# A hand-written order for the second layer, the last norms of the first layer beside it, and first transposes across row tiles

## The chip, the core and the metric

The kernel runs on one core of a Trainium2 chip. The metric is device time in microseconds (us) of one execution, and the median of several runs is quoted. Engines are named as in the profile: PE is the matrix engine (PEld its weight loads), DVE the vector engine, ACT the scalar (activation) engine, POOL the general engine, SP the engine that only issues transfers here. [...]

## What is computed

Two graph layers over N = 2708 nodes with 256 features in float32. The reference, cut to what matters:

```python
# layer 0: two steps (n = 0, 1), Xf = Xa = X at first
A  = top_p_attention(Xa, W1, W2, W3)      # row softmax, cut to the largest 90%, N x N
Xf = R @ Xf                               # R = (adj + I), rows scaled to sum 1: the "walk"
Xa = A @ Xa                               # the attention
Z  = Z + Xf @ U1[n].T + Xa @ U2[n].T
h  = X + Z;  layer0 = layernorm(h) * ln_g + ln_b
x  = layernorm(x + layer0)
# layer 1: graph attention with 4 heads of 64 features
Wh = einsum('nd,hdo->nho', x, W)          # values
e  = leaky_relu(s_i[:, None] + s_j[None]) # from Wh and a
P  = softmax over j of e where adj[i, j] != 0 (diagonal always)
x  = layernorm(x + einsum('ijh,jho->iho', P, Wh))
```

## The kernel before

**Row tiles.** The 2708 rows are cut into NT = 22 tiles: 16 of 128 rows and 6 of 110. Inside an attention row they are taken in six `groups` (four of 4 tiles with 128 rows, then 4 and 2 tiles with 110 rows).

**Layer 0** (`fast_layer0`, its main part from L1073) is written in an order fixed by hand: inside `tc.manual_schedule` the instructions of PE, ACT, DVE and POOL keep the order of the program. `step(s, ...)` runs over the 22 row tiles of step s. For each one `weigh` (L202) multiplies the attention row tile `e` with the values: for every group it transposes the group's blocks of `e` (L212, on PE), copies them from PSUM to SBUF (L218, on ACT, tile `eT`), and multiplies (L227, tile `att`). The transposes of group n+1 are issued ahead of the matmuls of group n, so that the copy has time; at the start of each row tile, though, groups 0 and 1 are transposed one after the other and the first matmul follows at once. After each group `slot` is called. A slot advances the searches under way (`search`: scores, threshold, candidates, the kept part of `e`, which ends with the DVE instruction of L805), may begin the search of the tile three further on, advances the small chains in `doing`, and pays out `spend` matmuls of the walk (L863). In step 0 spend is 0; in step 1 it is 6 or 7 for each slot. Between the steps thirteen slots of 7 walk matmuls start the searches of step 1.

**The end of a row in layer 0** is `finish` (L931): four sums on POOL into a tile `hh`, then two layernorms (bn_stats and bn_aggr on DVE, L948 and L949; epsilon and power on POOL, L952 and L953; scaling on DVE, L955), with gain, bias and residual on POOL between them (L961 to L963). Then `sources` transposes the row (L141), multiplies it with the weights of layer 1 (L147) and makes the factors `sb`, `tj`, `s_src` and the values `v`, which go to DRAM. Each `yield` in these generators hands over to the next slot.

**The verdict** (L1090 to L1134) is a chain of some 20 small DVE instructions on [128, 22] tiles that tests whether the fast search was exact. It ends in one PE matmul (L1131) and a flag `bad`, read at the very end.

**Layer 1** (`layer1`, L1145) has no order by hand; a planner places its instructions. The 22 target tiles are taken in three spans g (8, 8 and 6 tiles, 1024, 1024 and 660 columns). For each span it runs over all 22 source tiles j. One j is: load a block of the adjacency (L1170), ACT Sign and Square (L1171, L1176) to make a 0/1 mask, for a j inside the span two POOL operations on the diagonal block (L1174, L1175), four DVE instructions, one for each head, that give the weights `pt` (L1233), and on PE eight matmuls with 64 columns for the values (L1241) and eight with 32 columns for the denominators (L1248). `pt` has two buffers for each head. At the end of a span the sums go to SBUF (`val`, `den`), and `settle` (L1179) is called while the next span is at its third j: for all 8 (6) tiles of the span in one go, transposes (L1186, L1187), reciprocal (L1189) and product with it (L1193) on DVE, the residual on POOL (L1198), and `layernorm` (L124 to L132).

Of the kernel before, what the change touches and what calls it, by code (L numbers as in the profile page):

```python
# [8 lines left out]
F32 = mybir.dt.float32  # L9
BF16 = mybir.dt.bfloat16  # L10
I32 = mybir.dt.int32
AF = mybir.ActivationFunctionType
# [32 lines left out]
def kernel(  # L45
# [69 lines left out]
    bad = const.tile([1, 1], I32, name="bad")  # L115

# [19 lines left out]
    def sources(t, pool, ps):  # L136

        m = rows[t]
        tp = ps.tile([P, 4, P], F32, name="tr")
# [5 lines left out]
        wp = ps.tile([P, 4, P], F32, name="tr").rearrange("p a b -> p (a b)")  # L145
# [14 lines left out]
        nc.sync.dma_start(vd[t][:m], vt[:m])  # L160

# [40 lines left out]
    def weigh(acc, e, m, value, pool, ps, copies, between=None):  # L202

        def turned(n):
            grp = groups[n]
            tr = ps.tile([P, 4, P], F32, name="tr")  # L210
            for q, t in enumerate(grp):
                nc.tensor.transpose(  # L212
                    tr[: rows[t], q, :m], e[:m, off[t] : off[t + 1]], ident[:m, :m]
                )
            eT = pool.tile([P, 4, P], F32, name="eT")
            copy = copies[n % len(copies)]
            k = rows[grp[0]]
            copy(eT[:k, : len(grp), :m], tr[:k, : len(grp), :m])  # L218
            return eT

        ahead = turned(0)
        for n, grp in enumerate(groups):
            eT = ahead
            if n + 1 < len(groups):
                ahead = turned(n + 1)
            for q, t in enumerate(grp):
                nc.tensor.matmul(  # L227
                    acc, eT[: rows[t], q, :m], value(t),
                    start=(t == 0), stop=(t == NT - 1),
                )  # L230
            if between:
                between(n)


    def general_layer0():
        with ExitStack() as l0:
# [6 lines left out]
            g_sb = w0.tile([P, D], F32, name="g_sb")  # L243
            b_sb = w0.tile([P, D], F32, name="b_sb")
# [8 lines left out]
            nc.scalar.dma_start(g_sb, ln_g.partition_broadcast(P))  # L253
            nc.scalar.dma_start(b_sb, ln_b.partition_broadcast(P))
# [153 lines left out]
            def attend(t, e, rden, cur, dst):  # L408

                m = rows[t]  # L410
                ac = ps_ac.tile([P, CHUNK], F32, name="ac")
                weigh(ac[:m, :D], e, m, lambda j: cur[: rows[j], j, 0:D],
                      tpp, ps_tr, [nc.scalar.copy])
                nc.scalar.activation(dst, ac[:m, :D], AF.Copy, scale=rden[:m])
# [74 lines left out]
            for t in range(NT):  # L489
                for _ in sources(t, rowp, ps_tr):  # L490
                    pass


    def fast_layer0(ep, adjp):
# [24 lines left out]
        g_sb = w0.tile([P, D], F32, name="g_sb")  # L519
        b_sb = w0.tile([P, D], F32, name="b_sb")  # L520
# [13 lines left out]
        nc.scalar.dma_start(g_sb, ln_g.partition_broadcast(P))  # L534
        nc.scalar.dma_start(b_sb, ln_b.partition_broadcast(P))
        def constant(name, value, width=1):
            c = w0.tile([P, width], F32, name=name)
            nc.gpsimd.memset(c, value)
            return c
# [5 lines left out]
        ones = constant("ones", 1.0)  # L545
        place = w0.tile([P, 8], F32, name="place")
        for k in range(8):
# [5 lines left out]
                constant(f"fact{s}{k}", v, NT)  # L553
# [5 lines left out]
        wants = w0.tile([P, NT, SEGS], F32, name="wants")  # L559
        haves = w0.tile([P, NT, SEGS], F32, name="haves")  # L560
# [263 lines left out]
        def walks():  # L824
# [16 lines left out]
            for n, (s, t, j0, j1) in enumerate(queue):  # L841
# [7 lines left out]
                if j0 == 0:  # L849
                    ac = ps_wk.tile([P, CHUNK], F32, name="walk")  # L850
                    ca = finp.tile([P, D], F32, name="ca", bufs=4)
# [79 lines left out]
        def finish(t, ac, ca, cb):  # L931
# [9 lines left out]
            hh = heldp.tile([P, D], F32, name="hh", bufs=4)[:m]  # L941
            nc.gpsimd.tensor_add(hh, ca[:m], cb[:m])
            nc.gpsimd.tensor_add(hh, hh, held.pop(t)[:m])
            nc.gpsimd.tensor_add(hh, hh, xw)
            yield
            for last in range(2):
                st, mv = small.tile([P, 6], F32, name="ln_st")[:m], small.tile([P, 2], F32, name="ln_mv")[:m]
                nc.vector.bn_stats(st, hh)  # L948
                nc.vector.bn_aggr(mv, st)  # L949
                yield  # L950
                ve, rs = new("ln_ve", m), new("ln_rs", m)
                nc.gpsimd.tensor_scalar(ve, mv[:, 1:2], LN_EPS, None, op0=ALU.add)  # L952
                nc.gpsimd.tensor_tensor(rs, ve, minus_half[:m], op=ALU.pow)  # L953
                yield
                nc.vector.tensor_scalar(  # L955
                    xt if last else hh, hh, mv[:, 0:1], rs, op0=ALU.subtract, op1=ALU.mult
                )
                yield
                yield
                if not last:  # L960
                    nc.gpsimd.tensor_mul(hh, hh, g_sb[:m])  # L961
                    nc.gpsimd.tensor_add(hh, hh, b_sb[:m])
                    nc.gpsimd.tensor_add(hh, hh, ca[:m])  # L963
                    yield
                    yield
            yield from sources(t, rowp, ps_tr)


        engines = {nc.tensor.engine, nc.scalar.engine, nc.vector.engine, nc.gpsimd.engine}
# [25 lines left out]
        def step(s, cur, spend):  # L995
            for t in range(NT):
                m = rows[t]
                e, rden = ready.pop(t)
# [7 lines left out]
                def between(n):  # L1006
                    last = n == len(groups) - 1
                    if last:
# [9 lines left out]
                    slot(spend[n], (s, t + 3) if last else None)  # L1018

                weigh(ac[:m, :D], e, m, lambda j: cur[: rows[j], j, 0:D],  # L1020
                      tpp, ps_tr, [nc.scalar.copy], between)
# [44 lines left out]
        with tc.manual_schedule(engines=engines):  # L1066
# [10 lines left out]
            for t in range(3):  # L1077
                for n in range(6):
                    slot(SPEND_BETWEEN, None if n else (1, t))
                    if t == 2:  # L1080
                        break
# [4 lines left out]

        good = small.tile([P, 2, NT], F32, name="good")
        for s, r in enumerate(sorted_):  # L1090
            z, nxt, most, above, left = facts[s]
            ok, more = good[:, s, :], small.tile([P, NT], F32, name="more")
            nc.vector.tensor_tensor(ok, most, nxt, op=ALU.is_le)
            nc.vector.scalar_tensor_tensor(
                ok, nxt, 0.0, ok, op0=ALU.is_gt, op1=ALU.mult
            )
            if s:
                nc.vector.tensor_tensor(wants, wants, haves, op=ALU.min)
                nc.vector.tensor_reduce(more, wants, axis=AX.X, op=ALU.max)
                nc.vector.scalar_tensor_tensor(  # L1100
                    ok, more, 8.0, ok, op0=ALU.is_le, op1=ALU.mult
                )

                nc.vector.tensor_tensor(more, most, nxt, op=ALU.is_equal)
                nc.vector.tensor_add(above, above, left)
                nc.vector.tensor_scalar(above, above, float(r), None, op0=ALU.is_lt)
                nc.vector.tensor_mul(more, more, above)
                nc.vector.scalar_tensor_tensor(
                    ok, more, 0.0, ok, op0=ALU.is_equal, op1=ALU.mult
                )  # L1110

                nc.vector.scalar_tensor_tensor(
                    ok, left, float(r), ok, op0=ALU.is_lt, op1=ALU.mult
                )
            else:
                nc.vector.tensor_add(more, above, left)
                nc.vector.scalar_tensor_tensor(
                    ok, more, float(r), ok, op0=ALU.is_equal, op1=ALU.mult
                )
            nc.vector.scalar_tensor_tensor(  # L1120
                ok, z, Z_LOW, ok, op0=ALU.is_gt, op1=ALU.mult
            )
            nc.vector.scalar_tensor_tensor(
                ok, z, Z_HIGH, ok, op0=ALU.is_lt, op1=ALU.mult
            )
        total = small.tile([P, 1], F32, name="total")
        nc.vector.tensor_reduce(
            total, good.rearrange("p s t -> p (s t)"), axis=AX.X, op=ALU.add
        )
        pt = ps_wk.tile([P, CHUNK], F32, name="walk")  # L1130
        nc.tensor.matmul(pt[0:1, 0:1], total, ones, start=True, stop=True)  # L1131
        nc.vector.tensor_scalar(
            bad, pt[0:1, 0:1], -1.0, float(2 * NT * P), op0=ALU.mult, op1=ALU.add
        )  # L1134
        l0.close()
        return ahead
# [7 lines left out]
    def layer1(ep, adjp, r):  # L1144
# [9 lines left out]
        first = list(range(GT, NT - 2)) + list(range(GT)) + [NT - 2, NT - 1]  # L1154
# [24 lines left out]
        def settle(g, val, den):  # L1179

            for t in spans[g]:
                m = rows[t]
                cols = slice(off[t] - off[spans[g][0]], off[t + 1] - off[spans[g][0]])
                u = ps_u.tile([P, H, P], F32, name="aux")
                for q in range(2):
                    nc.tensor.transpose(u[:m, q, :], val[:, q, cols], ident)  # L1186
                nc.tensor.transpose(u[:m, 2, :], den[:, cols], ident)  # L1187
# [132 lines left out]
```

## Time and profile before

| | |
|---|---|
| device time, median of 3 runs | 1656.84 us (1656.59 to 1657.43) |
| span of the profiled execution | 1655.3 us |
| busy: PE / DVE / ACT / POOL | 1577.3 / 1229.6 / 742.3 / 430.1 us |
| mean granted PE clock | 0.987 |
| layer 0, step 0: first to last L227 | 78.9 to 468.0 us |
| layer 0, step 1: first to last L227 | 531.4 to about 1253 us |
| first matmul of layer 1 (L1241) | 1274.29 us |
| last matmul of layer 1's sums ends | about 1630.5 us |
| last DVE instruction (L132) | 1645.10 us |

The span counts from the first instruction to the last. "Busy" counts the time in which at least one instruction of the engine was under way. In the PE rows of the time line a float32 matmul shows as two records, so "x16" is eight matmuls. A row of a time line gives the start in us, the length, the engine, the line of the kernel, the operation, output and inputs, and the number of instructions merged into it; "[idle before <-releaser]" is how long the engine had stood idle and whose end let it go on.

### The profile page before, as it was taken

Reading aid. Unit: us, or ns where it says so; the run is one execution under the profiler, and the core shown is the slowest. Engines: PE = TensorE matmul, PEld = TensorE weight load, DVE = VectorE, ACT = ScalarE, POOL = GpSimd, SP = SyncE. Lnnn points to the kernel's source line nnn. Section 1 sums busy time; section 2 is a strip of 40 time slices with the busy share of each in tenths; the row PEclk is TensorE's granted clock in tenths of the full one; section 3 lists DMA queues with packets and bytes.
Section 4 is the critical chain, followed back from the end, with each engine's and each line's share of the span. In section 5 each row is a group of like instructions: output and inputs, shape, how many; then the busy total and the mean of one; then the engine's idle time right before and its main releaser. Section 6 shows DMA issues by size and latency. Waiting matters only on the chain. (4 is left out here: it accounts for less than half of the span.)

```text
span 1655.3 us, 23835 instructions
## 1 busy us (share of the span) xinstructions
PE 1577.3 (95%) x8029; PEld 1035.8 (63%) x8029; DVE 1229.6 (74%) x3682; ACT 742.3 (45%) x1263; POOL 430.1 (26%) x908
## 2 busy tenths in 40 slices
PE   7999999999999999999999999999997999999894
PEld 3476667666677887787778877887773222222332
DVE  3676667666508877876888888987873999899795
ACT  3433444343335555455455655556524344243231
POOL 2200000000022223222225554455433030420313
PEclk9999999999999999999999999999997999999997
DMA  7200000000024333233333433433354333432231
GB/s 196 69 9 15 9 9 11 9 9 8 12 68 121 90 90 98 80 83 78 80 90 97 111 106 99 111 100 91 90 132 143 109 92 97 123 88 80 79 84 32
DMA packets 172493, 128.26 MB, mean 77 GB/s; under 512 B 44342, under 2 KB 161804, under 8 KB 172362
## 3 DMA queue, kind: packets, MB, share of 16 engines
q1 hardware_dynamic: 166442, 115.87, 26.0%
q0 software_dynamic: 3648, 9.26, 1.8%
q10 hardware_dynamic: 2272, 1.52, 0.3%
q8 instruction: 65, 1.06, 0.3%
q14 instruction: 66, 0.54, 0.1%
HBM read 111.78 MB, written 13.46 MB: 76 GB/s over the span
## 5 line engine op out<-in xcount | busy, mean ns | idle before, releaser
L218 ACT COPY eT<-tr 128x512 f32<-128x512 f32 (+5 forms) x264 | 137.7, 539 | 252.0 <-PE tr L212 251.5
L227 PE MATMUL att<-xm,eT 128*128 128x256 f32 (+3 forms) x968 | 229.3, 381 | 17.4 <-ACT eT L218 17.4
L656 ACT ACTIVATE junk<-e,minus,rth 128x2708 bf16<-128x2708 f32 (+1 forms) x88 | 232.8, 2646 | 14.6 <-POOL rth L688 13.7
L227 PE MATMUL att<-ba,eT 128*128 128x256 f32 (+3 forms) x968 | 232.9, 381 | 5.1 <-ACT eT L218 4.9
L1241 PE MATMUL acc<-pt,v 128*64 128x512 f32 (+3 forms) x1056 | 229.3, 555 | 5.7 <-DVE pt L1233 4.5
L863 PE MATMUL walk<-xe,blk 128*128 128x257 f32 (+3 forms) x968 | 223.8, 382 | 1.9 <-DVE xf L877 1.8
L863 PE MATMUL walk<-xm,blk 128*128 128x256 f32 (+3 forms) x968 | 221.8, 380 | 0.0
L1233 DVE SCALAR_TENSOR_TENSOR pt<-e,tj,blk 128x1024 f32<-128x1024 f32 (+3 forms) x176 | 186.5, 1117 | 29.3 <-PE acc L1248 12.5
L863 PEld LDWEIGHTS walk<-xe,blk 128*128 128x128 f32 (+3 forms) x968 | 177.3, 185 | 46.7 <-issue 13.7
L227 PEld LDWEIGHTS att<-xm,eT 128*128 128x128 f32 (+3 forms) x968 | 171.2, 186 | 44.7 <-ACT eT L218 22.2
L863 PEld LDWEIGHTS walk<-xm,blk 128*128 128x128 f32 (+3 forms) x968 | 177.8, 186 | 32.9 <-issue 4.9
L227 PEld LDWEIGHTS att<-ba,eT 128*128 128x128 f32 (+3 forms) x968 | 171.0, 186 | 32.6 <-ACT eT L218 10.2
L635 ACT ACTIVATE e<-lg 128x1024 f32<-128x1024 f32 (+1 forms) x132 | 121.0, 921 | 131.6 <-PE lg L631 131.3
L736 DVE MAX8 cand<-e 128x8 f32<-128x170 f32 (+1 forms) x352 | 89.7, 323 | 114.4 <-ACT e L635 114.3
L1241 PEld LDWEIGHTS acc<-pt,v 128*64 128x64 f32 (+1 forms) x1056 | 72.8, 138 | 158.3 <-issue 112.0
L212 PEld LDWEIGHTS tr<-ident,e 128*128 128x128 f32 (+3 forms) x968 | 113.6, 139 | 45.5 <-PE lg L631 14.5
L212 PE MATMUL tr<-ident,e 128*128 128x128 f32 (+3 forms) x968 | 139.4, 270 | 0.9 <-DVE e L805 0.5
L1171 ACT ACTIVATE blk<-blk 128x1024 f32<-128x1024 f32 (+3 forms) x66 | 63.1, 956 | 165.9 <-DMA blk<-in_adjT_dram 159.5
L1248 PE MATMUL acc<-pt,sb 128*32 128x512 f32 (+3 forms) x1056 | 123.6, 548 | 0.0
L1233 DVE SCALAR_TENSOR_TENSOR pt<-r,tj,blk 128x1024 f32<-128x1024 f32 (+1 forms) x88 | 110.6, 1314 | 8.2 <-issue 5.5
L736 DVE MAX8 cand<-scr 128x8 f32<-128x97 f32 (+1 forms) x616 | 101.7, 244 | 0.0
L877 DVE TENSOR_TENSOR xf<-walk,xe 128x257 f32<-128x257 f32 (+1 forms) x22 | 9.4, 426 | 112.4 <-PE walk L863 112.4
(197 smaller groups left out, 1941.0 us busy)
## 6 DMA issues: line engine op xcount, KB each, us to landing
blk<-in_adjT_dram SPq DMA_DIRECT2D x32, 704.0 KB
blk<-in_adjT_dram SPq DMA_DIRECT2D x32, 512.0 KB
blk<-in_adjT_dram SPq DMA_DIRECT2D x48, 330.0 KB
blk<-in_adjT_dram SPq DMA_DIRECT2D x32, 320.0 KB
blk<-in_adjT_dram SPq DMA_DIRECT2D x12, 605.0 KB
blk<-in_adjT_dram SPq DMA_DIRECT2D x12, 440.0 KB
blk<-in_adjT_dram SPq DMA_DIRECT2D x18, 283.6 KB
c<-cs POOLq DMA_DIRECT2D x32, 128.0 KB, 2.0
```

What stands on the lines that cost most here:

```text
L212: nc.tensor.transpose(tr[: rows[t], q, :m], e[:m, off[t] : off[t + 1]], ident[:m, :m])
L218: copy(eT[:k, : len(grp), :m], tr[:k, : len(grp), :m])
L227: nc.tensor.matmul(acc, eT[: rows[t], q, :m], value(t), start=(t == 0), stop=(t == NT - 1),)
L635: nc.scalar.activation(halves[:m, :, c0 : c0 + w], lg[:m, :, :w], AF.Exp, accum_out=zp[:m, n : n + 1],)
L656: nc.scalar.activation(junk[:m], e[:m], func, scale=rth, bias=minus1[:m], accum_out=acc)
L736: nc.vector.max(cand[:, n, :], src[:m, n * size : min(N, (n + 1) * size)])
L863: nc.tensor.matmul(ac[:m, :w], blk[: rows[j], j - j0, :m], cur[: rows[j], j, 0:w], start=(j == 0), stop=(j == NT - 1),)
L877: nc.vector.tensor_add(xf[:m], ac[:m, : D + 1], xe[:m, t, :])
L1171: nc.scalar.activation(bar, bar, AF.Sign)
L1233: nc.vector.scalar_tensor_tensor(pt[:k, :gw], r[h // 2][:k, h % 2, :gw], tj[:k, j, h : h + 1], mask, op0=ALU.max, op1=ALU.mult,)
L1241: nc.tensor.matmul(acc[h // 2][c][q * FO : (q + 1) * FO, :w], v[j][:k, h - 1 + q, :], pts[h - 1 + q][:k, c0 : c0 + w], **at,)
L1248: nc.tensor.matmul(acc[2][c][h * 32 : (h + 1) * 32, :w], sb[:k, j, h : h + 1].to_broadcast([k, 32]), pts[h][:k, c0 : c0 + w], **at,)
```

## The change

1. **First transposes across row tiles.** `weigh` is given a function `turn_next`. Ahead of the matmuls of a tile's last group it transposes group 0 of the next row tile. To have that tile's `e` in time, a search begins one slot earlier in the tile, and two more slots (7 walk matmuls each) stand between the two steps.
2. **Layer 1 in a fixed order on all engines.** The whole of `layer1` runs inside `tc.manual_schedule`. The order runs over (span, j) in one line: masks two j ahead, weights one j ahead, also across the span's end.
3. **Settling spread out.** One row tile every second j, cut into four pieces that go to consecutive j; the product with the reciprocal goes from DVE to four ACT instructions with 64 columns each, except for the last span, whose six tiles use four freed accumulator banks beside the two `aux` ones. `val` and `den` are copied by ACT for the first 512 columns and by DVE for the rest.
4. **The last norms of layer 0 beside the first sums.** For the last LATE = 4 tiles the two norms and `sources` are taken out of layer 0 and advanced piece by piece in the first j of span 0, whose order puts these four tiles last. Their residual is kept in `x_late`; the norms work in place on `xe`.
5. **The verdict** is issued inside layer 1, after j number 17 of span 1.
6. Gain and bias are loaded first of all rather than behind the other weights, and some constants live in a pool that stays.

```diff
+    g_sb = const.tile([P, D], F32, name="g_sb")
+    nc.scalar.dma_start(g_sb, ln_g.partition_broadcast(P))
...
+    LATE = 4
+    x_late = const.tile([P, LATE, D], F32, name="x_late")
...
-        ahead = turned(0)
         for n, grp in enumerate(groups):
-            eT = ahead
-            if n + 1 < len(groups):
-                ahead = turned(n + 1)
+            eT, ahead = ahead, turn_next(n + 1)
...
-            hh = heldp.tile([P, D], F32, name="hh", bufs=4)[:m]
...
+            nc.gpsimd.tensor_add(xt, ca[:m], cb[:m])
+            nc.gpsimd.tensor_add(xt, xt, xw)
+            nc.gpsimd.tensor_add(xt, xt, held.pop(t)[:m])
+            if t < NT - LATE:
                 yield
+                yield from norms(t, ca)
+                yield from sources(t, rowp, lambda: ps_tr.tile([P, 4, P], F32, name="tr"))
...
-                    slot(spend[n], (s, t + 3) if last else None)
+                    slot(spend[n], (s, t + 3) if n == len(groups) - 2 else None)
+                def turn_next(n):
+                    u = t + n // len(groups)
+                    if u == NT:
+                        return None
+                    return turned(ready[u][0], rows[u], n % len(groups), tpp, ps_tr, nc.scalar.copy)
...
-                    if t == 2:
+                    if (t, n) == (2, 2):
                         break
...
+            if last:
                 nc.vector.tensor_tensor(
-                    res[:m], u[:m, 0:2, :].rearrange("p q (h o) -> p (q h) o", h=2),
-                    rden[:m].unsqueeze(2).to_broadcast([m, H, FO]), op=ALU.mult,
-                )
+                    res[:m], sums, rden[:m].unsqueeze(2).to_broadcast([m, H, FO]), op=ALU.mult
+                )
+            else:
+                for h in range(H):
+                    nc.scalar.activation(
+                        res[:m, h, :], sums[:, h, :], AF.Copy, scale=rden[:m, h : h + 1]
+                    )
+            yield
...
+        late = [prepared(t) for t in range(NT - LATE, NT)] if verdict else []
+        rest, running = [], []
+        mask(0)
+        mask(1)
+        weights(0)
+        for n, (g, i, j) in enumerate(order):
+            mask(n + 2)
+            for part in late[: n + 1]:
+                if next(part, late) is late:
+                    late.remove(part)
+            for part in list(running):
+                if next(part, running) is running:
+                    running.remove(part)
+            if rest and i >= 2 and i % 2 == 0:
+                running.append(settle(*rest.pop(0)[:4], aux(), False))
+                next(running[-1])
...
+            weights(n + 1)
...
+            for k in range(2):
+                values(n, (2 * k, 2 * k + 1))
...
+            denominators(n)
...
+            if verdict and (g, i) == (1, 3 * NT // 4 + 1):
+                verdict(aux()[0:1, 0, 0:1])
...
+        left = fast_layer0(ep, adjp)
+        with tc.manual_schedule(engines=engines):
+            layer1(ep, adjp, *left)
```

## The prediction

> **What bounds the kernel now.** I read the 40 slices first: where is PE, the busiest engine (95%), not full?
>
> ```profile
> PE   7999999999999999999999999999997999999894
> PEclk9999999999999999999999999999997999999997
> ```
>
> PE is short in the first slice, in slice 31 (1242 to 1283 us, between the layers) and at the end; slice 31 and the last also lose clock. The rest reads 9, but matmuls overlap, so a 9 can hide a slow stretch. So second, PE's waits, taken apart at 530 us (first answer step 0, second step 1):
>
> ```profile
> PE att L227 <- ACT eT L218: 17.4, 21, 1.0
> ```
> ```profile
> PE att L227 <- ACT eT L218: 4.9, 20, 0.4
> ```
>
> These are 21 and 20 waits: one at each row tile's start. The time line of PE, then of ACT, at one of them:
>
> ```profile
> 203.22 1.09 PE L212 MATMUL tr<-ident,e 128*128 128x128 f32 x8
> 205.18 1.99 PE L227 MATMUL att<-xm,eT 128*128 128x256 f32 x8 [0.87 <-ACT eT L218]
> ```
> ```profile
> 202.53 1.02 ACT L635 ACTIVATE e<-lg 128x1024 f32<-128x1024 f32 x1 [0.66 <-PE lg L631]
> ...
> 203.55 1.02 ACT L635 ACTIVATE e<-lg 128x1024 f32<-128x1024 f32 x1
> ...
> 204.54 1.07 ACT L218 COPY eT<-tr 128x512 f32<-128x512 f32 x2
> ```
>
> Groups 0 and 1 are transposed together and nothing else is left for PE, while ACT has two exponentials ahead of the copy. Third, the time line of PE between the layers:
>
> ```profile
> 1251.95 1.03 PE L227 MATMUL att<-ba,eT 110*110 110x256 f32 x4
> ...
> 1263.27 0.60 PE L141 MATMUL tr<-ident,xe 110*128 110x110 f32 x2 [4.92 <-DVE xe L955]
> ...
> 1269.93 0.60 PE L141 MATMUL tr<-ident,xe 110*128 110x110 f32 x2 [3.53 <-DVE xe L955]
> ...
> 1274.29 6.50 PE L1241 MATMUL acc<-pt,v 128*64 128x512 f32 x16 [1.23 <-ACT cs L157]
> ```
>
> From 1252.98 to 1274.29 (21.3 us) PE waits for the norms of the last tiles, one after the other. Fourth, layer 1: steady j's, then span 1 while span 0 is settled:
>
> ```profile
> 1304.32 3.65 PE L1241 MATMUL acc<-pt,v 128*64 128x512 f32 x16
> 1307.90 1.92 PE L1248 MATMUL acc<-pt,sb 128*32 128x512 f32 x16
> 1309.76 3.65 PE L1241 MATMUL acc<-pt,v 128*64 128x512 f32 x16
> ```
> ```profile
> 1415.35 0.41 PE L1186 MATMUL aux<-ident,val 128*128 128x128 f32 x2 [0.48 <-DVE res L1193]
> ...
> 1428.13 1.93 PE L1241 MATMUL acc<-pt,v 128*64 128x512 f32 x4 [1.45 <-DVE pt L1233]
> ```
> ```profile
> 1315.34 4.87 DVE L1233 SCALAR_TENSOR_TENSOR pt<-e,tj,blk 110x1024 f32<-110x1024 f32 x4 [0.57 <-ACT blk L1171]
> ```
>
> A steady j takes 1309.76 - 1304.32 = 5.44 us on PE without a gap, and DVE is done in 4.87, so PE is the bound and DVE has 0.57 to spare. In span 2 (time line) a j takes 3.62 on PE and 3.36 on DVE. The stretch with the settling is slower: j 2 of span 1 begins at 1407.63 and j 7 at 1450.99, 43.4 us for five j's that need 27.2.
>
> [...] PE is busy 39.94 of 42 us in 1407 to 1449, with 177 records where 1324 to 1366 has 252. [...] clock 0.50 from 1260 to 1278, and the first 16 records of L1241 take 6.50 us rather than 3.65. [...] beside the two POOL operations of a diagonal block four L1233 take 5.07 to 5.16 us rather than 4.87, and POOL's L1174 takes 1.10 beside 0.46 for L1175.
>
> **The change, part by part.**
>
> *A, step 0.* The two matmuls of the old tile's last group (about 0.95 us by the time line) and the scores of the next slot (0.76) now come between transposing group 0 and using it: 1.7 us more, more than the 0.87 missing. The copy still stands behind the two exponentials: they end about 3.3 us after the scores begin, the copy at 3.9, PE comes to it at about 4.5. 17.4 becomes about 1: -16.5.
>
> *B, step 1.* Seven walk matmuls (0.43 us each, 3.0) come in between as well: 4.9 becomes 0.4, -4.5. The risk is `e`: transposing earlier asks for it earlier. The search is moved by one slot too, and L805 ends 2.4 to 5.8 us before the transposes at the tile starts that I looked at (854.7 and 857.1; 722.5 and 728.4), so the shift by one short slot costs nothing. The two extra slots only move 14 walk matmuls forward: 0. Gain and bias loaded first: two issues of 0.4 us delay W1 by 0.8, its product is needed at 10.04 us but ready at 7.8: 0.
>
> *C, between the layers.* DVE's first L1233 started at 1253.08, right after the last attention matmul; two of them (1.28 each) let PE start. By the built order they stand directly behind the last DVE work of layer 0. 21.3 becomes 2.8[...]: -18.5.
>
> *D, moved PE work.* `sources` of four tiles goes into span 0: L141 0.3 and L147 0.9, 1.2 each, 4.8; 0.3 of it leaves layer 0: +4.5. The norms add at most two of three DVE pieces (bn 0.5, scaling 0.35) to a j, 0.85 against 0.57 spare, over eight j's; a j can be about 1.8 us late before PE sees it, because the last two heads are needed late. About 0.5, booked in E. Behind each waiting DVE piece stand the next four L1233, and PE behind those; but POOL has a whole j for its part.
>
> *E, stalls in layer 1.* The sums took 1630.52 - 1274.29 = 356.2 us. The need is 44 x 5.44 + 22 x 3.62 = 319.0, 16 settlings at 0.4 of PE (1407.63 to 1408.44 for two) 6.4, two shares 0.25 each: 325.9. So 30.3 us are stalls: 2.8 cold start, about 12.5 in span 1, 15 in span 2. Spread out, a settling costs DVE in two j's 0.15 + 0.5 + 0.35 = 1.0 us (L1193's 0.4 goes to four ACT instructions; the nearest row, L157, has 0.31 each, 1.2, beside 2.1 of masks in a j of 5.44) plus 0.15 to 0.4 for POOL's add, against a spare of 1.14 in span 1: nearly free. In span 2 the spare is 0.5, and PE gives 0.4 for its transposes: some 0.2 us each is left, 2 us with the diagonal blocks. Starting up 0.8, DVE's copies at two span ends 0.8, D's 0.5, other 0.3: 4.4 remain. -26.
>
> *F, verdict.* This adds a wait. By the built order PE has the verdict's matmul between j 17 and j 18 of span 1, and DVE has the 20 operations behind the weights of j 18. They end about when PE ends j 17, so PE stands idle for the chain: about 20 x 0.2 (before, L1112 and L1120 start 0.22 apart) = 4 us, all of PE queued behind it. [...] 0 to 3 us of slow clock, I take 1.5: +5.5, bounds 2 and 7.
>
> *G, the end.* From the last sum to the last L132 it took 15 us for six tiles, in pairs for want of `aux` banks. With six banks POOL sets the pace: 6 x (0.66 + 0.22 + 0.57 + gaps 0.2) = 9.9, and 1.6 to the first add, 0.5 for the last scaling: 12. -3. The 10 us to the span's end stay.
>
> Sum: -16.5 - 4.5 - 18.5 + 4.5 - 26 + 5.5 - 3 = -58.5; 1656.8 - 58.5 = **1598**.
>
> **The rivals.**
> - *DVE becomes the bound of layer 1.* For: it is within 10% of PE, and in a fixed order each of the 16 settlings may wait for POOL or PE, about 0.5 us, 8; the sums of span 2 (22 x 3.36, 8 x 1.4, 1.2, copies 1.9: 88.2 against 82.8 on PE) give 3.4 more than I booked. 1598 + 11.4 = 1610. Against: the waited-for work is one j old.
> - *A's gain fails*, because ACT has moved with it: the exponentials are begun one slot earlier and the copy stays behind them. My margin is 0.6 us. 1598 + 16.5 = 1614.
> - *Hardly a stall is left*: E gives all 30.3 and F costs 2: 1598 - 4.4 - 3.5 = 1590.
> - *Slower.* A wrong place in a fixed order repeats in every j: if DVE starts the weights of j+1 only when PE has finished j, each of 66 j's loses DVE's lead, about 2.44 us for two heads less what overlaps, say half: 80 us, 1678. For: two `pt` buffers bind DVE to PE closely. Against: they did so before, at 5.44.
>
> **How the numbers follow.** Likeliest 0.65, 1598; DVE 0.17, 1610; A fails 0.08, 1614; no stall 0.06, 1590; slower 0.04, 1678. The range runs from 1587 (no stall, and G and B at their best) to 1614; beyond it lie the slower case and part of the last rivals. Within 0.2% (3.3 us) no case falls: 0.01. Faster 0.95, slower 0.04.
>
> **What would show it.** Right: the waits of att for eT nearly gone; under 4 us from the last attention matmul to the first matmul of the values, at full clock; j's of 5.44 and 3.62 us through the settling; one PE wait of about 4 us in span 1 at the matmul of `ones` and `total`; 12 us at the end. Wrong: PE waiting for `pt` in many j's, a new wait of tr for `e` in step 1, or the clock low after the gap.

## The result, and the profile after

The changed kernel takes **1615.1 us** (median of 4 runs, 1614.56 to 1616.12) where the kernel before, beside it on the same chip, takes 1657.01. The ratio is 0.9748, with a 95% interval of 0.9731 to 0.9765. The forecast was 1598 with a range of 1587 to 1614: the direction was right, the gain was 42 us and not 58.5, and the time lies just outside the range.

The same two rows of 40 slices as for the kernel before, now of the changed one:

```profile
PE   6999999999998999999999999999999989998994
PEclk9999999999999999999999999999999999999997
```

The hole between the layers (slice 31 of before) is closed, and no slice but the last reads less than 9 for the clock; drops of a few us do not show in these digits (one follows below). What is new is an 8 in slice 13 (484 to 525 us), in slice 33 (1291 to 1332) and in slice 37 (1453 to 1493). PE's waits over the whole execution name them (total us, times, longest):

```profile
PE tr L607 <- DMA xa<-in_w1T_dram: 9.8, 1, 9.8
PE walk L893 <- DVE xf L907: 5.0, 3, 3.2
PE aux L1152 <- DVE total L1149: 4.5, 1, 4.5
PE acc L1283 <- DVE pt L1272: 3.7, 4, 2.1
...
PE att L258 <- ACT eT L245: 0.7, 2, 0.5
```

The 41 waits of att for eT, 22.3 us before, are down to two with 0.7 us. What is left is W1 at the start (9.8 us; it was 4.9), `xf` between the steps, the verdict's `total`, and `pt` in layer 1. The last row looks small, and that misleads: more is lost there than 3.7 us, as the next table shows. I made it from PE's time lines: the start of the first and the end of the last matmul of each stretch, in the profiled executions (spans 1655.3 and 1614.3 us; differences are of unrounded figures).

| stretch | before | after | difference | forecast |
|---|---|---|---|---|
| up to the first attention matmul | 78.9 | 82.9 | +4.0 | 0 |
| step 0 | 389.5 | 367.5 | -22.0 | -16.5 |
| between the steps, and step 1 | 784.6 | 780.1 | -4.5 | -4.8 |
| gap between the layers | 21.3 | 2.3 | -19.1 | -18.5 |
| layer 1, span 0 | 122.5 | 139.2 | +16.8 | |
| layer 1, span 1 | 135.8 | 130.4 | -5.4 | |
| layer 1, span 2 | 98.0 | 86.2 | -11.7 | |
| layer 1 together | 356.2 | 355.9 | -0.3 | -15.7 |
| after the last sum | 24.8 | 25.6 | +0.8 | -3 |
| sum | 1655.3 | 1614.3 | -41.0 | -58.5 |

(The forecast for layer 1 is D's 4.8, E's -26 and F's 5.5; D's other 0.3 is in the row of step 1.) So step 0 gave 5.5 us more than forecast and the gap 0.6 more, while the start (4.0), layer 1 (15.4, with span 0 as the stretch that grew) and the end (3.8) fell short by 23 us together. Some 17 us are missing in all.

**Layer 0.** PE at the start of a row tile in step 0:

```profile
199.60 0.66 PE L240 MATMUL tr<-ident,e 128*128 128x128 f32 x4
200.10 1.03 PE L258 MATMUL att<-xm,eT 110*128 110x256 f32 x4
201.06 0.82 PE L658 MATMUL lg<-junk,qT 64*128 64x330 f32 x4
```

The next tile's transposes (first row) are followed by the old tile's last matmuls and by scores; no bracket with a wait stands in the rows.

**Between the layers:**

```profile
1227.78 2.75 PE L258 MATMUL att<-ba,eT 110*110 110x256 f32 x12
1232.78 6.18 PE L1283 MATMUL acc<-pt,v 128*64 128x512 f32 x16 [2.25 <-DMA v<-v]
```

2.25 us instead of 21.3. The first 16 records still take 6.18 us rather than 3.65, for two reasons. The four products that feed them are made while they run, and DVE begins them only when PE has ended layer 0. And the clock was at half again: the profile's clock records read 0.50 from 1233.71 to 1237.12 us. Whether that happens changes from one profile to the next. These are the engines' busy times and then PEclk, DMA share and GB/s for 1230 to 1242 us, first of the changed kernel, then of one of the experiments below (the newest tile first at the end), which differs from it only behind this place and has the same gap (2.26 us):

```profile
1230.00:1242.00 12.00, 9.75 (x41) 2.80 (x41) 11.31 (x13) 1.58 (x3) 4.01 (x4) 0.86 0.74 226
```
```profile
1230.00:1242.00 12.00, 9.62 (x47) 2.85 (x48) 11.73 (x13) 2.56 (x3) 4.43 (x4) 1.00 0.77 233
```

The mean clock is 0.86 in one and 1.00 in the other, and j 0 takes 7.97 us in one and 6.94 in the other. So 1.0 of the 2.5 us that the changed kernel loses in j 0 goes with the slow clock. It is not lost in sum, though: j 3 and 4, where PE has caught up with DVE, take 12.72 us in the other kernel and 11.69 in this one.

**Span 0** is where the gain of the gap went. First DVE, then POOL, at j 6 to 8:

```profile
1265.94 4.87 DVE L1272 SCALAR_TENSOR_TENSOR pt<-e,tj,blk 128x1024 f32<-128x1024 f32 x4
1270.73 0.82 DVE L185 TENSOR_SCALAR xe<-xe,ln_mv,ln_rs 110x256 f32<-110x256 f32 x1
1273.04 0.43 DVE L177 BATCH_NORM_STATS2 ln_st<-xe 110x6 f32<-110x256 f32 x1 [1.50 <-POOL xe L192]
...
1273.60 6.27 DVE L1272 SCALAR_TENSOR_TENSOR pt<-e,tj,blk 128x1024 f32<-128x1024 f32 x4
```
```profile
1265.88 5.52 POOL L190 TENSOR_TENSOR xe<-xe,g_sb 110x256 f32<-110x256 f32 x1
...
1273.81 1.64 POOL L190 TENSOR_TENSOR xe<-xe,g_sb 110x256 f32<-110x256 f32 x1
1275.54 1.59 POOL L191 TENSOR_TENSOR xe<-xe,b_sb 110x256 f32<-110x256 f32 x1
```

L190 takes 0.6 to 0.7 us by itself. The first of the two rows has 5.52: it begins with DVE's four products and ends only after the last of them. DVE, whose next instruction in the fixed order is a norm that needs POOL's result, then stands idle for 1.50 us. After that both are under way at once, POOL's three operations take 1.6 us each, and DVE's four products 6.27 rather than 4.87. PE falls behind: j 7 of span 0 takes 9.98 us. One more wait has the same root. POOL's second operation on a diagonal block (L1197, 0.66 us in the median of its 22) takes 5.17 us beside four products at 1291.44; ACT's mask waits for it, behind the mask stands ACT's copy `xT`, and PE waits 1.9 us for that.

A second place in span 0 is j 14 and 15, 16.2 us for two. SP's queue, then ACT and PE:

```profile
1306.33 0.36 SPq L1192 DMA_DIRECT2D blk<-in_adjT_dram  x1
...
1312.01 6.58 SPq L223 DMA_DIRECT2D r<-shared  x4
1318.69 75.51 SPq L1192 DMA_DIRECT2D blk<-in_adjT_dram  x15
```
```profile
1326.27 1.06 ACT L1193 ACTIVATE blk<-blk 128x1024 f32<-128x1024 f32 x1 [13.05 <-DMA blk<-in_adjT_dram]
```
```profile
1330.86 1.07 PE L1283 MATMUL acc<-pt,v 128*64 128x512 f32 x2 [2.15 <-DVE pt L1272]
```

The mask of j 15 is issued only after the four loads that spread the next span's target weights (`spread`, 0.5 MB each), and ACT can take it 7.6 us later; for the mask of j 14, issued at 1306.33, it was 3.7.

The stalls of span 0 add up: 139.22 less 22 x 5.44 = 119.6 of sums, 4.8 of `sources` and 0.2 of `share` leaves 14.6. Of these, 2.5 lie in j 0, 6.8 in j 4 to 10 (49.8 us for seven j's), 5.3 in j 14 and 15.

**Span 1.** The settling costs nothing but PE's own transposes: pairs of j's take 11.35 us, 0.47 more than 10.88. The rest is the verdict:

```profile
1478.42 0.19 PE L1152 MATMUL aux<-ones,total 128*1 128x1 f32 x2 [4.45 <-DVE total L1149]
1478.54 5.79 PE L1283 MATMUL acc<-pt,v 110*64 110x512 f32 x16
```

4.45 us of waiting, then 5.79 rather than 3.65 us for the next matmuls, on an array that had gone slow (clock 0.50 from 1476.06 to 1482.88 us).

**The end.** DVE's last two scalings:

```profile
1601.84 0.72 DVE L1237 TENSOR_SCALAR o<-res,ln_mv,ln_rs 110x256 f32<-110x256 f32 x1 [1.00 <-POOL ln_rs L1234]
...
1604.11 0.41 DVE L1237 TENSOR_SCALAR o<-res,ln_mv,ln_rs 110x256 f32<-110x256 f32 x1 [1.00 <-POOL ln_rs L1234]
```

They are 2.27 us apart, with DVE idle ahead of each, waiting for POOL. POOL waits as well, 0.79 us for each tile:

```profile
1601.23 0.57 POOL L1234 TENSOR_TENSOR ln_rs<-ln_ve,minus_half 110x1 f32<-110x1 f32 x1
1601.77 0.64 POOL L1225 TENSOR_TENSOR res<-res,xe 110x256 f32<-110x256 f32 x1
1603.20 0.22 POOL L1233 TENSOR_SCALAR ln_ve<-ln_mv 110x1 f32<-110x1 f32 x1 [0.79 <-DVE ln_mv L1230]
```

### The profile page after: what moved, and what is told of

It reads as the page before. It is cut to its first block, busy times and chain, and to the rows that moved or that the text cites. A ratio compares the mean times of both kernels' runs of the same rounds, so it can differ in the third digit from the quotient of the medians.

```text
span 1614.3 us, 23771 instructions
## 1 busy us (share of the span) xinstructions
PE 1555.1 (96%) x8029; PEld 1032.9 (64%) x8029; DVE 1225.7 (76%) x3669; ACT 758.0 (47%) x1324; POOL 475.0 (29%) x908
## 4 chain that ended last, share of the span: by engine, by line
PE 83%; DVE 9%; DMA 3%; POOL 2%; ACT 1%; issue 1%; SPq 0%; ACTq 0%; POOLq 0%; DVEq 0%
PE att L258 25%; PE walk L893 24%; PE acc L1283 8%; PE lg L658 7%; PE tr L240 6%; DVE pt L1272 5%; PE acc L1293 4%; PE tr L938 2%; PE tr L952 2%; DMA blk<-in_adjT_dram 2%; PE tr L155 1%; PE lg L628 1%; PE tr L628 1%; DMA xa<-in_w1T_dram 0%; POOL blk L1197 0%
## 5 line engine op out<-in xcount | busy, mean ns | idle before, releaser
L245 ACT COPY eT<-tr 128x512 f32<-128x512 f32 (+5 forms) x264 | 141.5, 537 | 289.2 <-PE tr L240 286.4
L1272 DVE SCALAR_TENSOR_TENSOR pt<-e,tj,blk 128x1024 f32<-128x1024 f32 (+3 forms) x176 | 190.1, 1142 | 25.0 <-PE att L258 9.4
L240 PE MATMUL tr<-ident,e 128*128 128x128 f32 (+3 forms) x968 | 147.0, 271 | 0.3 <-ACT xe L944 0.3
L1293 PE MATMUL acc<-pt,sb 128*32 128x512 f32 (+3 forms) x1056 | 113.6, 548 | 0.0
```

The lines of the kernel that those rows point to most:

```text
L240: nc.tensor.transpose(tr[: rows[t], q, :m], e[:m, off[t] : off[t + 1]], ident[:m, :m])
L1272: nc.vector.scalar_tensor_tensor(pt[:k, :gw], targets[g][h // 2][:k, h % 2, :gw], tj[:k, j, h : h + 1], bar, op0=ALU.max, op1=ALU.mult,)
L1293: nc.tensor.matmul(acc[2][c][h * 32 : (h + 1) * 32, :w], sb[:k, j, h : h + 1].to_broadcast([k, 32]), probs[n][h][:k, c0 : c0 + w], **at,)
```

## Experiments

All times are medians; ratios are to the kernel before, run on the same chip beside them, with a 95% interval. Each kernel is the changed kernel with the edit shown. The parts not edited repeat from run to run within some tenths of a us, except in four places. All four stand behind a short wait of PE, after which the clock is at half for 3.4 us in some profiles and stays full in others:

- j 0 of span 0, after a gap of 2.1 to 3.2 us: 7.8 to 8.1 us in the five profiles with the slow clock, 6.7 to 7.3 in the five without;
- j 14 and 15, as long as the spreading loads stand together: 16.2 and 16.6 us with it, 13.2 to 14.5 without. Only 0.6 to 0.8 of this difference lies behind the drop (j 15 takes 8.3 to 8.5 rather than 7.7); the rest is a longer wait in j 14;
- j 4 to 10 where their work is that of the changed kernel: 51.7 us in two profiles with a slow clock in j 9 and 10, 49.8 to 50.0 in four without;
- j 17 and 18 of span 1, after the verdict: 16.6 to 16.8 us with 3.4 us of slow clock, 17.5 to 18.0 with 6.8.

A difference of a profile in those places says nothing by itself unless it is larger than that. Nothing in the runs shows what decides whether the clock drops after such a wait.

### The loads of gain and bias last

```diff
-    nc.scalar.dma_start(g_sb, ln_g.partition_broadcast(P))      # ahead of everything
-    nc.scalar.dma_start(b_sb, ln_b.partition_broadcast(P))
...
+        nc.scalar.dma_start(g_sb, ln_g.partition_broadcast(P))  # behind the last of u1T, u2T
+        nc.scalar.dma_start(b_sb, ln_b.partition_broadcast(P))
```

> The changed kernel (1615.1 us) with one edit: the loads of gain and bias are issued after all the other weights, as in the kernel before. Theory A (in the changed kernel these two loads stand ahead of W1 on the queue, and that is why PE first has W1 at 9.8 us rather than 4.9): W1 is there at about 5 us, the first attention matmul comes at 79 us rather than 82.9, and the time is 1611. Rival (the first products are bound by the loads of x, which are as slow for another reason): W1 comes earlier but the first attention matmul stays at 82 to 83, and the time at 1614 to 1615.

Measured: 1611.08 us (0.972, 0.9703 to 0.9736), 4.0 less. PE's first matmul and the first product of the projection (L628), which stood at 9.81 and 14.03 us:

```profile
5.00 0.61 PE L607 MATMUL tr<-ident,xa 128*64 128x128 f32 x2 [5.00 <-DMA xa<-in_w1T_dram]
...
10.16 3.78 PE L628 MATMUL lg<-ba,wkqk 128*128 128x512 f32 x4 [1.33 <-ACT ba L1082]
```

The first attention matmul comes at 79.01. The whole 4 us of the start are these two loads. They are two short issues (0.44 and 0.45 us), but 256 KB that go to all partitions ahead of W1's 64 KB. No run takes their size apart from their form (one line copied to 128 partitions). SP's six loads of x, on another queue, take longer beside them too: 10.8 us to issue in the changed kernel and 8.4 in this one.

### The verdict ahead of the first weights

```diff
+        if verdict:
+            verdict(aux()[0:1, 0, 0:1])
         mask(0)
         mask(1)
         weights(0)
...
-            if verdict and (g, i) == (1, 3 * NT // 4 + 1):
-                verdict(aux()[0:1, 0, 0:1])
```

> The changed kernel (1615.1) with one edit: the verdict is written ahead of the first weights of layer 1, not between j 17 and 18 of span 1. Theory A (its 20 DVE operations cost PE 4.45 us of waiting in span 1, and the idle array 2.1 us of slow clock after it; DVE is idle for 9.4 us before the first weights, so there they are free): span 1 takes 123.7 us rather than 130.4, the gap between the layers stays near 2.3, and the time is 1608.4. Rival (the verdict's facts, or its bank of PSUM, are there only when the last attention matmul has ended; the 4.4 us then delay the first weights): the gap grows to about 6.5 and the clock drops there, 1613 to 1615.

Measured: 1609.54 us (0.9711, 0.9695 to 0.9728). Span 1 takes 123.65 us rather than 130.42, the gap 2.56, and no wait for `total` is left. By these two profiles the verdict cost 6.8 us in the changed kernel (5.8 to 7.1 by the spread of j 17 and 18 above) and costs 0.3 here: DVE does it while it would wait for PE to end layer 0. The medians give 5.6.

### The spreading loads one at a time

```diff
                 nc.sync.dma_start(
                     r[k][:, h, :n].rearrange("p (t m) -> p t m", t=len(spans[g])),
                     lines[2 * k + h].partition_broadcast(P),
                 )
+                yield
...
-                spread(g + 1, targets[g + 1])
+                spreading = spread(g + 1, targets[g + 1])
+            if NT // 2 < i <= NT // 2 + 4 and g + 1 < len(spans):
+                next(spreading)
```

> The changed kernel (1615.1) with one edit: the four loads that spread the next span's target weights over the partitions (0.5 MB each) are issued one per j from j 12 to 15, not all four at j 11. Theory A (they stand ahead of the mask of j 15 of span 0 on the one queue of SP, 6.6 us to issue[...]; that is why DVE waits 6.7 us for this mask and PE loses 5.3 us in j 14 and 15): these two j's take 10.9 us rather than 16.2, and the time is 1609.8. Rival (the mask is late because ACT and POOL, which prepare it, are behind): the wait stays, 1614 to 1616; if each of the four loads delays a mask of its own, it gets worse, 1617.

Measured: 1611.92 us (0.9723, 0.9706 to 0.9739), 3.2 less; j 14 and 15 take 10.87 us, j 16 0.8 more than a steady one, and span 0 134.8. SP is not among the engines whose order is fixed: in its queue three of the four loads still stand together (issued from 1312.99 us on). But the mask of j 15 now goes ahead of them, at 1312.42 rather than 1318.69. ACT still takes it only 7.1 us after its issue (7.6 in the changed kernel), so the transfer itself is hardly faster. It was the place in SP's queue, then, not ACT or POOL.

### The late norms back in layer 0

```diff
-            if t < NT - LATE:
-                yield
-                yield from norms(t, ca)
-                yield from sources(t, rowp, ...)
+            yield
+            yield from norms(t, ca)
+            yield from sources(t, rowp, ...)
...
-        late = [prepared(t) for t in range(NT - LATE, NT)] if verdict else []
+        late = []
```

> The changed kernel (1615.1) with one part undone: the norms and the sources of the last four tiles stay in layer 0 (after the last attention matmul), and nothing of them lies beside span 0. Theory A (beside span 0 the norms cost DVE and POOL more than I booked: some 8.6 us of the 14.5 us that PE stalls there): the gap between the layers is 19 to 21 us again, with 2.8 us of slow clock behind it, and span 0 takes 126 us rather than 139.2 (4.8 of it is PE's own work that moves out, 8.6 stalls); the time is 1623. Rival (the norms are nearly free there, as I predicted, and the stalls of span 0 have other causes): span 0 takes about 133, and the time is 1631.

Measured: 1618.82 us (0.9766, 0.9749 to 0.9782). The gap is 18.0 us, and span 0 takes 124.9. In j 4 to 10 it takes 38.3 us where the changed kernel takes 49.8: 11.5, of which 4.8 are PE's own work and 6.7 stalls. So the stalls of j 4 to 10 come from the moved norms and `sources`; moving them saves 15.7 us at the gap and costs 11.5 in span 0. All of part 4 of the change is worth some 4 us (3.7 by the medians, 4.1 by the profiled spans). (My expectation put the slow clock after the gap at 2.8 us: the clock is 0.50 until 1254.3 us, and j 0 takes 7.55 us, 2.1 more than a steady one.)

### Each tile's first transposes at its own start

```diff
                 def turn_next(n):
-                    u = t + n // len(groups)
-                    if u == NT:
+                    if n == len(groups):
                         return None
-                    return turned(ready[u][0], rows[u], n % len(groups), tpp, ps_tr, nc.scalar.copy)
+                    return turned(e, m, n, tpp, ps_tr, nc.scalar.copy)
```

> The changed kernel (1615.1) with one part undone: each row tile transposes its own group 0 and 1 at its start, as before; the slots of the search stay where the change put them. Theory A (the waits of att for eT were all that the change took away in layer 0[...]): step 0 takes 389.5 us rather than 367.5, step 1 about 709 rather than 704.3, and the time is 1642. Rival (the recorded waits alone, 17.4 and 4.9 us less the 1.1 that are left): 1636. Second rival (the search that starts one slot earlier, not the transposes, made step 0 shorter): 1618.

Measured: 1643.42 us (0.9916, 0.9899 to 0.9933), 28.3 more. The time is as the first theory said, but the split is not. Step 0 takes 380.7 us, not 389.5, and PE waits less than before in it:

```profile
PE att L258 <- ACT eT L245: 7.8, 21, 0.4
```

The other edit of part 1, the search that begins a slot earlier, is still in this kernel. It moves the exponentials away from the tile's start, so that the wait falls from 17.4 to 7.8 us without the transposes: step 0 gains 8.8 from the slot and then 13.2 from the transposes. No run has the transposes without the slot, so the split holds for this order only. Between the steps and in step 1 the signs differ: 793.9 us here, 784.6 in the kernel before, 780.1 in the changed one. There the earlier slot and the two added ones, with what little else differs in layer 0, cost 9.3. PE waits 5.0 us rather than 1.8 for `xf` (I suppose because the walk runs further ahead of DVE), 3.4 us at half clock follow that, and att waits once for 3.1 us near the end of layer 0; its 19 other waits, 0.24 to 0.29 us each, are as before. The transposes then give 13.8, that one long wait included. Which part of the change makes PE wait longer for `xf` was not tested.

Per tile start the transposes give 13.2 / 21 = 0.63 us, of which 7.8 / 21 = 0.37 are on record as a wait. A stop in step 0 thus cost some 0.26 us more than its recorded wait, at full clock. The 0.26 is the sum of whatever is lost there; no run takes it apart.

### GpSimd's wide operations left out

```diff
-                nc.gpsimd.tensor_mul(hh, hh, g_sb[:m])
-                nc.gpsimd.tensor_add(hh, hh, b_sb[:m])
-                nc.gpsimd.tensor_add(hh, hh, xt[:m])
+                if not short:          # short: the late tiles
+                    nc.gpsimd.tensor_mul(hh, hh, g_sb[:m])
+                    nc.gpsimd.tensor_add(hh, hh, b_sb[:m])
+                    nc.gpsimd.tensor_add(hh, hh, xt[:m])
```

> The changed kernel (1615.1), where the norms of the last four tiles beside span 0 leave out GpSimd's three operations of 256 columns (times gain, plus bias, plus x); DVE's and PE's instructions are the same. Theory A ([...] these three stretch four products of weights from 4.85 to 5.7 to 6.3 us and themselves wait up to 5.5 us): of the 6.7 us of stalls in j 4 to 10 some 5 go, these seven j's take 45 us rather than 49.8, and the time is 1610. Rival (DVE's own added work, about 1.9 us a tile against 0.57 us to spare in a j, is what stalls): they still take 49 us, 1614.

Measured: 1609.42 us (0.971, 0.9691 to 0.973). The kernel leaves out gain, bias and residual of the late tiles, so only its time is of use (two runs). j 4 to 10 take 44.7 us rather than 49.8, with all of DVE's work in place: of the 6.8 us of stalls 5.1 went with twelve POOL instructions. So DVE's own added work accounts for at most the small rest; and 1.3 us of that rest are the wait for `xT` behind the diagonal block. The five groups of four products from 1252.73 us on take 4.85 to 4.87 us here, where the changed kernel has one of 5.68 (at 1253.86) and one of 6.27 (at 1273.60) among the five from there on, and DVE's 1.50 us of waiting for POOL are gone. The run takes out POOL's operations whole, their own 0.6 to 0.7 us as well as what they and DVE's products lose beside each other; that the latter is the larger part is read from those rows.

### Two late tiles

```diff
-    LATE = 4
+    LATE = 2
```

> The changed kernel (1615.1) with two late tiles rather than four: the norms and sources of tiles 18 and 19 stay in layer 0, where DVE is idle in the last 20 us before the last attention matmul; those of 20 and 21 stay beside span 0. Theory A (a late tile costs 1.7 us of stalls in span 0 and 1.2 us of PE's own work, which only moves): the stalls of j 4 to 10 fall from 6.7 to about 3.4, the gap between the layers stays under 3 us, 1611.7. Rival (the norms of tile 19 end only after the last attention matmul, so the gap grows by 3 to 5 us): 1615 to 1617. Second rival (the stalls come from four tiles at work at once, and two are nearly free): 1609.

Measured: 1605.85 us (0.9686, 0.967 to 0.9703), more than any theory gave. Of the 10.1 us by which span 0 is shorter, 3.1 lie in two of the places that vary anyway (j 0; j 14 and 15; the clock stayed full in both), 2.4 are PE's work that stays in layer 0 (whose step 1 is 1.5 longer), and 4.6 are stalls in j 4 to 10. So two tiles leave 2.2 us of stalls in j 4 to 10 where four leave 6.8: the cost grows faster than the number of tiles that are under way at once. The gap stays at 2.29. DVE is idle from 1213 to 1222 us there, so it had room there for the norms of tiles 18 and 19.

### The newest tile first at the end

```diff
         while rest or running:
-            for part in list(running):
+            for part in list(reversed(running)):
```

> The changed kernel (1615.1) with one edit in the last loop: of the tiles under way the newest is stepped first, so that GpSimd adds the next tile's sum before it takes the root of this one's variance. Theory A (the tail is a ring of DVE and GpSimd that waits for each other, 2.25 us a tile, not GpSimd's 1.45 us of work, which I had priced): a tile takes 1.6 to 1.7 us, the last scaling comes 12.5 us after the last sum rather than 15.9, and the time is 1612. Rival (the stores' queue sets the end: one store is issued each 2.1 us and lands some 10 us after): 1615.

Measured: 1610.35 us (0.9717, 0.9701 to 0.9733), 4.8 less. POOL's additions of two tiles in turn are now 1.57 us apart:

```profile
1592.80 0.72 POOL L1225 TENSOR_TENSOR res<-res,xe 110x256 f32<-110x256 f32 x1
...
1594.37 0.64 POOL L1225 TENSOR_TENSOR res<-res,xe 110x256 f32<-110x256 f32 x1
```

The last scaling ends 11.7 us after the last sum, where it took 15.9 in the changed kernel and 15.0 in the one before; the stretch after the last sum is 21.1 us rather than 25.6. The stores follow suit, so their queue was not the limit; only the last scaling waits 0.86 us for an earlier store.

### All five edits, with two late tiles and with one

The edits of the first three experiments, of the last one, and LATE at 2 or 1.

> The changed kernel (1615.1) with five edits at once: gain and bias loaded last, the verdict ahead of the first weights, the four spreading loads one per j, two late tiles rather than four, and the newest tile first in the last loop. Theory A (each edit takes away a different stop, so the gains add up): first attention matmul at 79, gap 2.4, span 0 in 127, span 1 in 123.7, span 2 in 86.1, the tail 21.1; together 1590 (4.0 + 5.6 + 3.2 + 9.3 + 4.8 = 26.9 less than the changed kernel by the times alone would be 1588). Rival (some share a cause: with two tiles the masks are no longer late, so spreading the loads gives nothing, or the verdict's operations now stand in DVE's way where the two more norms are): 1594 to 1597.

> The same five edits with only one late tile. Theory A (PE waits 2.3 us between the layers for the loads of v in any case, and the sources of tile 20 fit into that): the gap stays under 3 us, span 0 falls by another 1.2 us of PE's own work and about 1 us of stalls, 1588. Rival (the norms of tile 20 end only some 8 us after its attention result, with its sources 2 us behind, and everything waits for that): the gap grows by 2 to 5 us, 1590 to 1594.

Measured: 1590.12 us (0.9599, 0.9583 to 0.9615) and **1587.37 us** (0.9582, 0.9566 to 0.9598). The five gains nearly add up: 25.0 of the 26.8 us that the five runs alone show together. With one late tile the gap is 3.17 us, 0.6 more than with two, since PE waits for the tile 20 that stays in layer 0, but span 0 takes 122.9 rather than 126.4, and 0.7 us of stalls are left in j 4 to 10. The clock records of both profiles show no drop in layer 1 before the end. The slices of the fastest:

```profile
PE   7999999999998999999999999999999999999995
PEclk9999999999999999999999999999999999999998
```

The 8 that is left is the wait for `xf` between the steps (3.2 us in one piece) with the slow clock behind it (513.2 to 516.7 us); its cause is left open.

## Why the forecast was right and where it failed

Three steps of the sum failed: the norms beside span 0 (D and E, the main one), the loads of gain and bias (B, the start) and the pace of the end (G). A wait for a mask is missing from it. Step 0 gave more than forecast and hid 5.5 us of what all this cost.

**A, step 0: right mechanism, too small.** The waits are gone as worked out. The gain is 22.0 and not 16.5 because I took the recorded waits for the cost of the stops; the difference is 0.26 us for each of 21 stops. Nor was the account whole: the slot that alone gave 8.8 of the 22 was booked at nothing.

**B, step 1: right sum, wrong parts.** The two stretches together gave 4.5 of 4.8. But "the two extra slots only move 14 walk matmuls forward: 0" and "the shift by one short slot costs nothing" stand for a cost of 9.3 us, which the transposes, with 13.8 rather than 4.5, happened to outweigh.

**The start: the step that failed** is "two issues of 0.4 us delay W1 by 0.8". I priced the issue and not the transfer of 256 KB that it asks for. W1 came 4.9 us later, the first attention matmul 4.0.

**C, the gap: right in size**, 19.1 of 18.5. But the sign that I gave, full clock behind the gap, did not come: after 2.25 us the clock was at half for 3.4 us in the changed kernel. That it would stay full was my estimate; in the trace of before it does after a wait of 2.50 us (PE before 1558.34 us; the clock reads 1.00 from 1280.1 to 1635).

**D and E, span 0: the main failure.** The step is "about 0.5, booked in E" for the norms beside the sums. They cost 6.8 us of stalls besides PE's 4.8. I compared DVE's added work with its spare time, and wrote that POOL has a whole j for its part. It has not: I had the rows that show DVE's products and POOL's operations slower beside each other (four products 5.07 to 5.16 us rather than 4.87, L1174 1.10 us) and did not use them for POOL's side. Here it was worse: four DVE products of 1.2 us stand back to back, and L190 took 5.52 us, past the end of all four (4.87), while DVE's order puts a norm that needs it next. Removing three POOL instructions per tile gives back 5.1 of the 6.8.

A second term of span 0 is missing altogether: the mask behind the spreading loads, 5.3 us in the profiled run. The fixed order keeps only two masks ahead and puts four loads of 0.5 MB into SP's queue between two of them; the planner of before had issued these loads while the first j was running at half clock (at 1276.25 us; the clock was 0.50 until 1280.05). Starting up took 2.5 us, not 0.8, with the slow clock in it.

**E, spans 1 and 2: right.** Without the verdict span 1 stalls nowhere; a settling takes 0.47 us of PE rather than 0.4. Span 2 keeps 2.8 us of stalls, of which I had 2 (settlings and diagonal blocks).

**F, the verdict: right**, 6.8 for a forecast of 5.5 with bounds of 2 and 7. The chain took 4.45 us for the 4 worked out, the slow clock 2.1 for 1.5. The 1.5 was my estimate. In the changed kernel this wait of 4.45 us was followed by 6.8 us at half clock, and the gap of C, 2.25 us, by 3.4.

**G, the end: failed.** "With six banks POOL sets the pace" counted POOL's work, 1.65 us a tile. The order written out makes a ring: POOL's root, then its addition for the next tile, then DVE's statistics of it, then the root of that. A tile takes 2.27 us, and the end is 0.8 us longer than before. Reversing one loop gives 1.57 us, close to the 1.65 that I had assumed.

Of the rivals, "A's gain fails" (1614) comes nearest in time, by accident: A gave more than forecast, not nothing. "DVE becomes the bound of layer 1" (1610) has the right stretch for another reason: it blamed the settlings, which cost nothing but PE's transposes, and not the norms of span 0.

With the five edits the kernel takes 1587 to 1590 us. That is below the 1598 of the forecast, so it doesn't confirm the sum: the edits also take out the verdict's cost, which the forecast had booked, and one of them keeps more tiles in layer 0.

## What to carry to other kernels

When work is moved beside a busy engine, count what its partner needs at the same time: here a chain that goes back and forth between DVE and GpSimd beside back-to-back DVE products waited for whole groups of them (5.52 us beside four of 1.2 us), and the fixed order passed that on to all that stood behind. In a fixed order, look for idle time that is there already (here DVE's before the first weights of layer 1) before putting small chains into a full loop, and list the queues whose order is not fixed, with the bytes that each issue asks for. For a chain that runs around two engines, price the ring and not the busier engine.

## What the runs showed of the hardware

- A GpSimd operation that takes 0.6 to 0.7 us took 5.52 us beside four DVE instructions of 1.2 us in a row: it ended only after the last of them. A second one, of 0.66 us in the median, took 5.17 us beside such a group; in the run without GpSimd's wide operations a small one, of 0.23 us in the changed kernel's median (L182), took 5.07. When both were in step, DVE's group of four took 6.27 us rather than 4.87 and GpSimd's operations 1.6 us each.
- In step 0, 21 stops of PE with 0.37 us of recorded wait each cost 0.63 us each, 0.26 more than the profile records.
- After a gap of 2.25 us the clock was at half for 3.4 us in one profile (first j 7.97 us); after one of 2.26 us it stayed full in another (6.94 us).
- Two loads of 128 KB to all partitions, 0.9 us to issue, delayed a load of 64 KB behind them by 4.9 us at the start, beside the loads of x.
